# Row maxima of attention scores: at every second split tile, scores of key differences go through ScalarE before VectorE reduces them, and two sets of keys are kept, not three

## The chip, the cores and the metric

The kernel runs on one core of one Trainium2 chip. The metric is the device time of one execution in microseconds (us). The engines are called PE (TensorE's matmuls), PEld (its weight loads), DVE (VectorE), ACT (ScalarE), POOL (GpSimd) and SP (SyncE, which issues the DMAs).

## The reference

The input `x` is 8 sequences of 1024 tokens with 256 features, all in fp32. The work is one attention layer and one feed-forward layer, each with a layer norm before it, a layer norm after it and a residual:

```python
x = x + _layernorm(_L0_attn_ref(_layernorm(x), Wq, Wk, Wv, Wo))
x = x + _layernorm(_L0_ffn_ref(_layernorm(x), weight, alpha, bias))
# attention: 16 query heads and 4 key/value heads of 16 features, rotary embedding on q and k
scores = jnp.einsum('bhqd,bhkd->bhqk', q, k) / jnp.sqrt(jnp.float32(D))
p = jax.nn.softmax(scores, axis=-1)
o = jnp.einsum('bhqk,bhkd->bhqd', p, v)
```

What matters here is the softmax. Its row maximum has to be known before the exponentials are taken, so every score is computed twice: once to find the maximum of its row, and once, shifted by that maximum, for the exponential.

## The kernel before, in words

**Units and blocks.** The kernel walks through 16 units (half a sequence of queries, 512 tokens, index `u`; two units make a sequence `b`). A unit has 4 blocks (index `i`, 64 in all) and a block has 8 steps of 4 exponentials. A unit is thus 32 steps or 128 exponentials, and the kernel has 2048 exponentials.

**The two score streams.** For an exponential, PE writes a 128x512 tile `se` of scores (L655), ACT takes `Exp` of it into `e` (L671), and PE multiplies `e` with `v_aug` into `av` (L691). `se` tiles come from a pool of 3 PSUM banks, which the products of projections and tails share. For the maxima, PE writes score tiles `sm` (L582, in `max_scores`); one holds 2 x 512 scores of 128 queries, one half for each half of the keys, and spans two PSUM banks. There are 2 such tiles in turn. DVE reduces a tile with `TENSOR_REDUCE` (L607, in `reduce_halves`) into `mx`. The maxima run 13 steps ahead of the exponentials. When a block has its maxima, DVE joins them (`mc`, L624), PE transposes them (`pm`, L630), ACT and DVE split them (`mh`, `ml`, L632 and L639), and a DMA writes them as extra rows into the stacked queries `q_st` (L646), so that the second score product comes out shifted.

**Windows.** The order on PE, DVE and ACT is written by hand, in windows (`window`, from L1114). A window has 3 exponentials, or 2 where a part of the projection or of the tail with a PSUM product of its own is ready. For each exponential PE also does one half of an `sm` tile (a pair of matmuls, one `se` and one `sm`). After the pairs come the part's product, if any, and the `av` products of the window before the last. A window that ends after the first half of an `sm` tile leaves a split tile: `reduce_early` (L612) has DVE reduce the first half by itself at the end of the window, and the second half is reduced by itself after the first pair of the next window. So a whole tile is one `TENSOR_REDUCE` of 128x1024, and a split tile is two of 128x512.

**Projections and keys.** While unit `u - 3` runs, unit `u` is projected: `kv_and_dram` makes keys and values and sends the keys through DRAM into another layout; `kt` rotates them on POOL, splits them into a high and a low part, writes them to DRAM (`dk`) and at once calls `stack_keys`, whose six DMAs load them into `k_st` (L481). There are three sets of `k_st` and `v_aug`, one for each sequence in turn. `v` fills `v_aug`. `P_PARTS` (L942) lists at which step each part stands. DMAs are issued by SP in an order that a scheduler chooses.

**Tail.** The last unit's tail uses `k_st` and `v_aug` of finished sequences as scratch.

Of the kernel before, what the change touches and what calls it, by code (L numbers as in the profile page):

```python
# [16 lines left out]
P = 128  # L17
# [5 lines left out]
UQ = UT * P  # L23
EPS = 1e-5
THRESH_FACTOR = 0.7


@with_exitstack
def kernel(
# [103 lines left out]
    k_st, v_aug, q_st = [], [], []  # L133
    for i in range(2):
        q_st.append(const.tile([P, G, 2, UQ], F32R, name=f"q_st{i}"))
    for i in range(3):
        k_st.append(const.tile([P, 2, S], F32R, name=f"k_st{i}"))
        v_aug.append(const.tile([P, NK, HKV, 32], F32, name=f"v_aug{i}"))

# [10 lines left out]
    def fill_constant_parts(i):  # L150
        if i > 0:
            fill_rows(k_st[i], 1, NROW, 64 - NROW)
        nc.gpsimd.memset(v_aug[i], 1.0)

    def split_hi(eng, hi, src):
# [149 lines left out]
    class Project:  # L305
# [54 lines left out]
        def v(self):  # L360

            lo = 0 if self.u < 2 else DK
            pt = psum([P, UT, P], f"ptv_{self.u}")
            for t in range(UT):
                src = self.kv_t[lo:, t * P : (t + 1) * P]
                nc.tensor.transpose(pt[:, t, lo:], src, ident[lo:, lo:])
            if lo == 0:
                self.k_rot = qkp.tile([P, UT, DK], F32, tag="k_rot", name=f"k_rot_{self.u}")
                nc.scalar.copy(self.k_rot, pt[:, :, :DK])
            if self.u == 0:  # L370
                self.split_q(0, (0,))
            nc.scalar.copy(
                v_aug[self.b % 3][:, self.half * UT : (self.half + 1) * UT, :, 0:HD],
                pt[:, :, DK:].rearrange("p t (r d) -> p t r d", d=HD),
            )

# [30 lines left out]
        def kv_and_dram(self):  # L407

            u = self.u
            for p in range(2):  # L410
                self.kv(p)
            d_k = dram.tile([DK, UQ], F32, tag="d_k", name=f"d_k_{u}")
            nc.sync.dma_start(out=d_k, in_=self.kv_t[:DK])
            self.k_rot = qkp.tile([P, 2, P], F32, tag="k_rot", name=f"k_rot_{u}")
            src = d_k.rearrange("(m e) (g t) -> e g m t", e=2, t=P)
            for e in range(2):
                nc.sync.dma_start(out=self.k_rot[:, e, :], in_=src[e])

        def kt(self):
            rotate(  # L420
                self.eng, self.k_rot, cos_kt_sb[:, self.half], sin_kt_sb[:, self.half],
                work.tile([P, 2, P], F32, tag="t2k", name=f"t2k_{self.u}", bufs=1),
            )
            hl = qkp.tile([P, 2, 2, P], F32R, tag="k_parts", name=f"ks_{self.u}")
            split(self.eng, hl[:, 0], hl[:, 1], self.k_rot)
            dk = self.dk = dram.tile([2, DK, UQ], F32, tag="dk", name=f"dk_{self.u}")
            dst = dk.rearrange("l (m e) (g t) -> l e g m t", e=2, t=P)
            for l in range(2):
                for e in range(2):
                    nc.sync.dma_start(out=dst[l, e], in_=hl[:, l, e, :].bitcast(F32))  # L430
            self.stack_keys()

        def q_product(self, p):
            if self.q_rot is None:
# [36 lines left out]
                    src = self.hl["q"][64 * c : 64 * (c + 1), l].rearrange("p e t -> p (e t)")  # L471
                    nc.sync.dma_start(out=rows[l, c], in_=src.bitcast(F32))

        def stack_keys(self):

            keys = slice(self.half * UQ, (self.half + 1) * UQ)
            src = self.dk.rearrange("l (r a d) t -> a l d r t", a=2, d=HD)
            for a in range(2):
                for band, l in enumerate((0, 0, 1)):
                    row = 64 * a + HD * band  # L480
                    nc.sync.dma_start(  # L481
                        out=k_st[self.b % 3][row : row + HD, :, keys].bitcast(F32), in_=src[a, l]
                    )

    def row_pickers():

# [75 lines left out]
    def head_and_tile(i, r2, t):  # L562
        return r2 * UT + t if i // G < NU - 1 else 2 * t + r2

    def max_scores(v):


        i, k = divmod(v // 2, 2 * NK)
        u, part = i // G, v % 2
        if i == 0:  # L570
            a, ch, t, r2 = 1 - part, k // NK, k // 2 % UT, k % 2
        else:
            a, ch, t, r2 = 1 - k % 2, part, k // 4, k // 2 % 2
        queries = block_queries(i, r2)
        queries = queries[:, t * P : (t + 1) * P] if u < NU - 1 else queries[:, t]
        if part == 0:
            sm[0] = ps_mx.tile([P, 2, 512], F32, tag="sm", name=f"sm_{i}_{k}")
            if k == 0:
                mx[i] = small.tile([P, 2, 2 * UT, 2], F32, tag="mx", name=f"mx_{i}")
            reduced.clear()  # L580
        rows = slice(64 * a, 64 * a + 64)
        scores = nc.tensor.matmul(  # L582
            sm[0][:, part, :],
            queries[rows],
            k_st[(u // UPB) % 3][rows, r2, ch * 512 : (ch + 1) * 512],
            start=True,
            stop=True,
        )
        if part == 0:
            return  # L590
        if reduced:
            tc.declare_no_dep(scores.ins, early[0], reason="another bank")
        if i == 0:
            nc.vector.tensor_reduce(
                mx[i][:, ::-1, head_and_tile(i, r2, t), ch], sm[0], AX.X, ALU.max
            )
        else:
            reduce_halves(i, k, 2)
        if k == 2 * NK - 1:
            shift_join(i)  # L600
            due.append((v // 4 + (1 if i < 3 else 2), i))
# [10 lines left out]
    def reduce_early(v):  # L612

        i, k = divmod(v // 2, 2 * NK)
        if i > 0 and v % 2:
            reduce_halves(i, k, 1)

    sm, mhl, shifts, reduced, early = {}, {}, {}, [], [None]
# [32 lines left out]
    def exp_scores(n, r2, a, sc):  # L651
        i, kt = divmod(n, NK)
        queries = block_queries(i, r2)
        rows = slice(64 * a, 64 * a + 64)
        nc.tensor.matmul(  # L655
            sc if len(queries.shape) == 2 else sc.rearrange("p (j t) -> p j t", j=G),
            k_st[(i // G // UPB) % 3][rows, r2, kt * P : (kt + 1) * P],
            queries[rows],
            start=True,
            stop=True,  # L660
        )
# [20 lines left out]

    def av_piece(i, first, end):

        va = v_aug[(i // G // UPB) % 3]
        if first == 0:
            av_ps[0] = ps_av.tile([P, UQ], F32, tag="av", name=f"av_{i}")
        for kt in range(first // UQ, (end - 1) // UQ + 1):
            lo, hi = max(first - kt * UQ, 0), min(end - kt * UQ, UQ)
            for r in (1, 2, 3, 0):  # L690
                nc.tensor.matmul(  # L691
                    av_ps[0][32 * r : 32 * r + 32, lo:hi],
                    va[:, kt, r, :],
                    es[i * NK + kt, r // 2, r % 2][:, lo:hi],
                    start=(kt == 0 and lo == 0),
                    stop=(kt == NK - 1 and hi == UQ),
                )
# [140 lines left out]
    class LastTail(Tail):  # L838
# [4 lines left out]
        def __init__(self, u):  # L843
            super().__init__(u)
            self.xn = qkp.tile([P, UT, D], F32, tag="xn", name="xn_last", bufs=2)

        def new(self, what, p):
            i = (B - 3) % 3 if what == "x1" else (B - 2) % 3
            if what == "xn":
                return self.xn[:, p : p + 1]  # L850
            if what == "hl":
                tile = k_st[i][:, p // 2, (p % 2) * 2 * D : (p % 2 + 1) * 2 * D]
                return tile.rearrange("p (l t d) -> p l t d", l=2, t=1)
            return v_aug[i][:, 2 * p : 2 * p + 2].rearrange("p t r d -> p (t r d)").unsqueeze(1)
# [82 lines left out]
    def load(u):  # L937
# [3 lines left out]

    P_PARTS = (  # L942
        (26, "begin", 0), (33, "x", 0, 0), (34, "x", 0, 1), (37, "begin", 1), (43, "x", 1, 0),
        (45, "x", 1, 1), (49, "kv_and_dram"), (51, "q", 0), (52, "kt"), (53, "v"), (55, "q", 1),
        (57, "q_to_dram"),
    )
    L_PARTS = (
        (10, "n", 0), (13, "o", 0), (15, "attn", 0), (16, "stats_a", 0), (19, "stats_x", 0),
# [8 lines left out]
        (29, "x", 1, 1), (31, "ffn", 1), (31, "stats_f", 0), (33, "stats_f", 1),  # L957
    )

    P_FIRST = (47, 51, 52, 54, 57, 58, 59, 60, 62, 61, 63, 64)  # L960
    T_LAST = (1, 3, 4, 5, 9, 10, 11, 14, 17, 20, 21, 21, 22, 24, 25, 26, 23, 27)

    warm = []
# [13 lines left out]
    def third(name, *args):  # L977
        return lambda: getattr(projects[2], name)(*args)
# [6 lines left out]
    for k, fs in enumerate((  # L985
# [16 lines left out]
        [third("v"), second("split_q", 1), second("q_to_dram")],  # L1002
        [],
        [],
        [(fill_constant_parts, 2)],
        [],
        [third("q", 0)],
        [(behind_shift, 1, third("kt"))],
# [2 lines left out]
    )):  # L1011
        for f in fs:
            at(k - START, *(f if isinstance(f, tuple) else (f,)))
    for u in range(3, NU):
        start = SPU * (u - 4)
        steps = P_FIRST if u == 3 else [k for k, *_ in P_PARTS]
# [6 lines left out]
                at(k, stage)  # L1023
        at(start + steps[0] - 1, begin_project, u)
        for k, (_, *p) in zip(steps, P_PARTS):
            at(start + k, part, projects, u, *p)
    for u in range(2, NU):
        at(SPU * (u - 1) + 1, stack_queries, u)
    for u in range(NU - 1):
# [63 lines left out]

    def start_step(n):
        for q in range(4):
            max_scores(maxima[0])
            maxima[0] += 1
            if q == 1:
                take_low()
        collect(n)  # L1100
        do_parts(99)
# [12 lines left out]
    def window(s):  # L1114
# [8 lines left out]
        else:  # L1123
            end = min(maxima_by(s + size), 4 * NSTEP)
            for q in range(max(size, end - maxima[0])):
                if q < size:
                    exp_one(s + q)
                if maxima[0] < end:
                    max_scores(maxima[0])
                    maxima[0] += 1  # L1130
                if q == 0:
                    take_low()
# [143 lines left out]
```

## Time and profile before

| what | value |
|---|---|
| median of 3 runs | 1645.67 us (1642.97 to 1648.71) |
| profiled execution: time, span | 1642.63 us, 1640.8 us |
| granted TensorE clock, mean | 0.989 |
| busy share of the span: PE, DVE, ACT, POOL | 96%, 85%, 78%, 51% |
| `TENSOR_REDUCE` of 128x1024 / 128x512 (L607) | 712 / 592 |
| exponentials (L671) | 1996, mean 602 ns |

A row of the groups gives line, engine, operation, output and inputs, shape and count; then busy time in us and the mean duration of one in ns; then the engine's idle time just before them and what ended it. A row of the timeline gives start and duration in us; rows of one kind that follow each other are merged, with their count. A busy PE is not a PE at its peak, since matmuls are pipelined. The 52 exponentials that stand under another line belong to the end of the kernel, where no maxima are left.

### The profile page before, as it was taken

Reading aid. Unit: us, or ns where it says so; the run is one execution under the profiler, and the core shown is the slowest. Engines: PE = TensorE matmul, PEld = TensorE weight load, DVE = VectorE, ACT = ScalarE, POOL = GpSimd, SP = SyncE. Lnnn points to the kernel's source line nnn. Section 1 sums busy time; section 2 is a strip of 40 time slices with the busy share of each in tenths; the row PEclk is TensorE's granted clock in tenths of the full one; section 3 lists DMA queues with packets and bytes.
Section 4 is the critical chain, followed back from the end, with each engine's and each line's share of the span. In section 5 each row is a group of like instructions: output and inputs, shape, how many; then the busy total and the mean of one; then the engine's idle time right before and its main releaser. Section 6 shows DMA issues by size and latency. Waiting matters only on the chain.

```text
span 1640.8 us, 37250 instructions
## 1 busy us (share of the span) xinstructions
PE 1579.7 (96%) x14712; PEld 818.5 (50%) x14712; DVE 1399.3 (85%) x2049; ACT 1274.8 (78%) x2479; POOL 835.4 (51%) x1239
## 2 busy tenths in 40 slices
PE   7999999999999999999999999999999999999997
PEld 5544455454545545454544545455454544444544
DVE  7778788889898888989889898988989888898964
ACT  4657778878787887878788787887878787877884
POOL 5532457374653737455373835547374552323363
PEclk8989999999999999999999999999999999999999
DMA  4151425125151422515133251513325151231100
GB/s 139 53 101 34 91 77 101 59 76 101 56 106 49 91 67 82 101 46 105 60 83 75 77 106 44 104 49 89 71 67 104 40 97 42 46 70 34 42 15 27
DMA packets 86079, 117.99 MB, mean 72 GB/s; under 512 B 12088, under 2 KB 50808, under 8 KB 85752
## 3 DMA queue, kind: packets, MB, share of 16 engines
q1 hardware_dynamic: 85904, 115.60, 29.9%
q8 instruction: 116, 1.90, 0.5%
q14 instruction: 59, 0.48, 0.1%
HBM read 68.65 MB, written 45.88 MB: 70 GB/s over the span
## 4 chain that ended last, share of the span: by engine, by line
PE 80%; DVE 10%; DMA 3%; ACT 2%; POOL 2%; issue 2%; SPq 1%; POOLq 0%; DVEq 0%; ACTq 0%
PE av L691 28%; PE se L655 28%; PE sm L582 9%; DVE mx L607 7%; PE pa L283 3%; PE pq L283 2%; PE pf L283 2%; PE pt_ot L267 2%; ACT e L671 2%; PE pt_xt L267 2%; PE pkv L283 2%; DMA q_st<-ml 1%; DMA k_rot<-d_k 1%; PE pm L630 1%; DMA dk<-ks 1%
## 5 line engine op out<-in xcount | busy, mean ns | idle before, releaser
L607 DVE TENSOR_REDUCE mx<-sm 128x2 f32<-128x1024 f32 (+1 forms) x1304 | 1205.3, 973 | 191.9 <-PE sm L582 174.1
L671 ACT ACTIVATE e<-se 128x512 f32<-128x512 f32 x1996 | 1058.2, 602 | 223.0 <-PE sm L582 172.4
L582 PE MATMUL sm<-k_st,q_st 64*128 64x512 f32 x2048 | 748.4, 450 | 6.9 <-DVE mx L607 3.9
L655 PE MATMUL se<-q_st,k_st 64*128 64x512 f32 x2048 | 705.5, 441 | 26.7 <-ACT e L671 14.4
L691 PE MATMUL av<-e,v_aug 128*32 128x256 f32 (+3 forms) x8608 | 607.2, 378 | 0.0
L655 PEld LDWEIGHTS se<-q_st,k_st 64*128 64x128 f32 x2048 | 324.9, 185 | 405.7 <-ACT e L671 302.1
L582 PEld LDWEIGHTS sm<-k_st,q_st 64*128 64x128 f32 x2048 | 326.1, 185 | 65.1 <-DVE mx L607 41.9
L691 PEld LDWEIGHTS av<-e,v_aug 128*32 128x32 f32 x8608 | 194.4, 108 | 211.0 <-issue 148.3
L241 POOL TENSOR_SCALAR lnsc<-mv 128x2 f32<-128x2 f32 (+1 forms) x134 | 25.8, 193 | 400.1 <-DVE mv L239 395.1
L765 POOL TENSOR_TENSOR xn<-xn,a 128x512 f32<-128x512 f32 x30 | 38.4, 1282 | 131.8 <-DMA a<-d_rec 101.2
L826 POOL TENSOR_TENSOR a<-a,bias_bc 128x512 f32<-128x512 f32 x30 | 38.6, 1287 | 108.3 <-ACT a L825 108.3
L242 POOL TENSOR_TENSOR lnsc<-lnsc,mhalf 128x2 f32<-128x2 f32 (+1 forms) x134 | 92.5, 691 | 0.9
L162 POOL TENSOR_TENSOR hl<-xn,hl 128x512 fp32r<-128x512 f32 x60 | 76.5, 1287 | 0.4
L253 POOL TENSOR_SCALAR xn<-x,lnsc 128x256 f32<-128x256 f32 x116 | 65.1, 570 | 2.2
L237 DVE BATCH_NORM_STATS2 bnst<-a 128x6 f32<-128x256 f32 x120 | 44.5, 413 | 4.6 <-POOL a L826 4.6
L297 POOL TENSOR_TENSOR t<-q_rot,sin_q_sb 128x512 f32<-128x512 f32 x31 | 39.9, 1288 | 15.5 <-ACT q_rot L439 15.4
L283 PE MATMUL pa<-woh,hl 128*128 128x256 f32 x240 | 46.2, 294 | 1.1 <-ACT e L671 1.1
L283 PE MATMUL pq<-xt,wqkvh 128*128 128x256 f32 x256 | 45.8, 303 | 0.5 <-ACT e L671 0.5
L237 DVE BATCH_NORM_STATS2 bnst<-x 128x6 f32<-128x256 f32 x124 | 45.9, 412 | 0.4 <-DMA x<-in_L_attn_x 0.4
L271 ACT CAST ot<-pt_ot 128x512 fp32r<-128x512 f32 x66 | 39.6, 601 | 4.7 <-PE pt_ot L267 4.7
L439 ACT COPY q_rot<-pq 128x512 f32<-128x512 f32 x32 | 18.8, 586 | 30.9 <-PE pq L283 30.9
L162 POOL TENSOR_TENSOR hlq<-q_rot,hlq 128x512 fp32r<-128x512 f32 x31 | 39.8, 1285 | 4.8 <-ACT hlq L159 4.5
(157 smaller groups left out, 1303.1 us busy)
## 6 DMA issues: line engine op xcount, KB each, us to landing
q_st<-dq SPq DMA_DIRECT2D x90, 256.0 KB
dq<-hlq SPq DMA_DIRECT2D x60, 256.0 KB
d_av<-avsb SPq DMA_DIRECT2D x60, 256.0 KB
x<-in_L_attn_x SPq DMA_DIRECT2D x15, 512.0 KB
xn<-d_av SPq DMA_DIRECT2D x30, 256.0 KB
a<-d_rec SPq DMA_DIRECT2D x30, 256.0 KB
xr<-in_L_attn_x SPq DMA_DIRECT2D x15, 512.0 KB
out_x<-a SPq DMA_DIRECT2D x30, 256.0 KB
```

Of the source, the lines that this page charges most:

```text
L162: eng.tensor_tensor(lo, src, hi.bitcast(F32), ALU.subtract)
L237: nc.vector.bn_stats(st[:, t, :], src[:, t, :])
L242: nc.gpsimd.tensor_tensor(sc[:, 1, :], sc[:, 1, :], mhalf[:, :n], ALU.pow)
L253: eng.tensor_scalar(dst[:, t, :], src[:, t, :], sc[:, 0, t : t + 1] if eng is nc.gpsimd else mv[:, t, 0:1], sc[:, 1, t : t + 1], ALU.add i ...
L267: nc.tensor.transpose(pt[:, c, t * P : (t + 1) * P], src[:, t, c * P : (c + 1) * P], ident_r)
L283: nc.tensor.matmul(out, chunk(left[i], c), chunk(right[j], c), start=(k == 0), stop=(k == len(steps) - 1),)
L297: eng.tensor_tensor(dst, x, table.unsqueeze(1).to_broadcast(list(x.shape)), ALU.mult)
L582: scores = nc.tensor.matmul(sm[0][:, part, :], queries[rows], k_st[(u // UPB) % 3][rows, r2, ch * 512 : (ch + 1) * 512], start=True, stop= ...
L607: early[0] = nc.vector.tensor_reduce(mx[i][:, a, head_and_tile(i, r2, t), lo:n], sm[0][:, lo:n, :], AX.X, ALU.max).ins
L655: nc.tensor.matmul(sc if len(queries.shape) == 2 else sc.rearrange("p (j t) -> p j t", j=G), k_st[(i // G // UPB) % 3][rows, r2, kt * P : ...
L671: nc.scalar.activation(e, sc, AF.Exp, scale=1.0 / D**0.5)
L691: nc.tensor.matmul(av_ps[0][32 * r : 32 * r + 32, lo:hi], va[:, kt, r, :], es[i * NK + kt, r // 2, r % 2][:, lo:hi], start=(kt == 0 and lo ...
```

## The change

Of the split tiles, every second one takes another way, for blocks of sequences 1 to 7 apart from each sequence's first block. Its first half is not the scores with the first half of the keys: it is the scores with `k_df`, the keys of the second half minus those of the first. Its second half is the scores with the first half of the keys. ACT takes the positive part (`Relu`) of the first half into an SBUF tile `rest` at the end of the window, behind the window's exponentials, and in place of both reductions DVE adds `rest` to the second half and takes the maximum of the sums in one instruction, since max(s0, s1) = s0 + relu(s1 - s0).

`k_df` is made on POOL once a sequence, from the rotated keys of both units (`k_differences`), goes through DRAM as the keys do (`dkd`), and is loaded by six DMAs 9 steps before the exponentials reach the sequence (`stack_differences`). To have room for `k_df` and `rest`, `k_st` and `v_aug` have two sets. So `stack_keys` is no longer called by `kt`: it stands at its own step, 68, as `v` does at 67, when the set's former sequence is done. `kt` stands at 54. `kt`, `q_to_dram`, `stack_keys` and `stack_differences` are issued behind the latest shift rows' DMA. Each `mx` tile is first filled by POOL with a large negative number, as only one of its two columns is written for such a tile. The last tail gets a tile of its own for `x1`.

```diff
+    k_df = const.tile([P, 2, S // 2], F32R, name="k_df")
-    for i in range(3):
+    for i in range(2):
         k_st.append(const.tile([P, 2, S], F32R, name=f"k_st{i}"))
...
+        def k_differences(self):
+            first = projects[self.u - 1].k_rot
+            self.eng.tensor_tensor(first, self.k_rot, first, ALU.subtract)
+            self.dkd = self.k_to_dram("dkd", first)
...
+    def maxima_tile(i):
+        if i < NU * G and i not in mx:
+            mx[i] = small.tile([P, 2, 2 * UT, 2], F32, tag="mx", name=f"mx_{i}")
+            nc.gpsimd.memset(mx[i], LEAST)
...
-    def max_scores(v):
+    def max_scores(v, end):
...
+            if v + 1 == end and u >= UPB and i % (UPB * G) > 0:
+                sm["turn"] = not sm.get("turn", False)
+                if sm["turn"]:
+                    sm["rest"] = work.tile([P, 512], F32, tag="rest", name=f"rest_{i}_{k}")
+                    keys = k_df
+        elif sm["rest"] is not None:
+            keys = k_st[(u // UPB) % 2][:, :, :512]
...
-        if reduced:
+        if reduced or sm["rest"] is not None:
             tc.declare_no_dep(scores.ins, early[0], reason="another bank")
...
+        elif sm["rest"] is not None:
+            rest, x = sm["rest"], head_and_tile(i, r2, t)
+            nc.vector.tensor_tensor_reduce(
+                rest, sm[0][:, 1, :], rest, 1.0, LEAST, ALU.add, ALU.max, mx[i][:, a, x, 0:1]
+            )
...
-        if i > 0 and v % 2:
+        if v % 2 and sm["rest"] is not None:
+            early[0] = nc.scalar.activation(sm["rest"], sm[0][:, 0, :], AF.Relu).ins
+        elif i > 0 and v % 2:
             reduce_halves(i, k, 1)
...
-        (45, "x", 1, 1), (49, "kv_and_dram"), (51, "q", 0), (52, "kt"), (53, "v"), (55, "q", 1),
-        (57, "q_to_dram"),
+        (45, "x", 1, 1), (49, "kv_and_dram"), (51, "q", 0), (54, "kt"), (55, "q", 1),
+        (57, "q_to_dram"), (67, "v"), (68, "stack_keys"),
...
+    at(8 - START + 10, third("stack_keys"))
+    for u in range(3, NU, UPB):
+        at(SPU * (u - 4) + (66 if u == 3 else 55), part, projects, u, "k_differences")
+        at(SPU * (u - 1) - 9, behind_latest, part, projects, u, "stack_differences")
```

## The prediction

> **What bounds the kernel now.** I read the page first: busy shares, then the chain that ended last.
>
> ```profile
> PE 1579.7 (96%) x14712; PEld 818.5 (50%) x14712; DVE 1399.3 (85%) x2049; ACT 1274.8 (78%) x2479; POOL 835.4 (51%) x1239
> ...
> PE 80%; DVE 10%; DMA 3%; ACT 2%; POOL 2%; issue 2%; SPq 1%; POOLq 0%; DVEq 0%; ACTq 0%
> ```
>
> PE is on the chain for most of the time; DVE has a tenth of it, ACT almost nothing. DVE is busier than ACT, but neither is full. So a DVE microsecond is worth something only where PE waits for it. The groups by shape give the prices, and a row of the waits (us in sum, times, longest) tells who stands for whom:
>
> ```profile
> L607 DVE TENSOR_REDUCE mx<-sm 128x2 f32<-128x1024 f32 x712 | 855.3, 1216 | 167.5 <-PE sm L582 153.2 <-PE se L655 11.0
> L607 DVE TENSOR_REDUCE mx<-sm 128x1 f32<-128x512 f32 x592 | 381.9, 680 | 24.5 <-PE sm L582 20.9
> ...
> L639 DVE SCALAR_TENSOR_TENSOR ml<-mh,low,pm 32x128 fp32r<-32x128 f32 x64 | 21.0, 327 | 3.1 <-ACT mh L632 3.1
> ...
> L162 DVE TENSOR_TENSOR xs<-xn,xs 128x512 fp32r<-128x512 f32 x3 | 3.1, 1045 | 0.0
> ...
> L797 DVE TENSOR_TENSOR v_aug<-v_aug,xr 128x256 f32<-128x256 f32 x3 | 1.3, 426 | 0.1
> L881 DVE TENSOR_TENSOR xn_last<-po,rec 128x256 f32<-128x256 f32 x3 | 1.3, 425 | 0.1
> ...
> L510 DVE TENSOR_SCALAR low<-low 32x1 f32<-32x1 f32 x1 | 0.1, 142 | 0.0
> ```
>
> ```profile
> PEld sm L582 <- DVE mx L607: 41.9, 127, 1.4
> ...
> PE se L655 <- DMA q_st<-ml: 9.9, 8, 3.1
> ```
>
> Last the timeline, engine by engine, at one split tile between two windows of three. This is the place where the change acts:
>
> ```profile
> 687.58 1.20 DVE L607 TENSOR_REDUCE mx<-sm 128x2 f32<-128x1024 f32 x1
> 688.72 1.20 DVE L607 TENSOR_REDUCE mx<-sm 128x2 f32<-128x1024 f32 x1
> 689.85 0.67 DVE L607 TENSOR_REDUCE mx<-sm 128x1 f32<-128x512 f32 x1
> 690.62 0.69 DVE L607 TENSOR_REDUCE mx<-sm 128x1 f32<-128x512 f32 x1
> 691.23 1.21 DVE L607 TENSOR_REDUCE mx<-sm 128x2 f32<-128x1024 f32 x1
> ...
> 688.65 1.62 ACT L671 ACTIVATE e<-se 128x512 f32<-128x512 f32 x3
> 690.59 3.27 ACT L671 ACTIVATE e<-se 128x512 f32<-128x512 f32 x6 [0.32 <-PE sm L582]
> ...
> 688.84 0.50 PE L582 MATMUL sm<-k_st,q_st 64*128 64x512 f32 x1
> ...
> 690.05 0.73 PE L582 MATMUL sm<-k_st,q_st 64*128 64x512 f32 x2
> ...
> 692.50 0.49 PE L582 MATMUL sm<-k_st,q_st 64*128 64x512 f32 x1
> ```
>
> The third pair's `sm` half at 688.84 starts 0.06 us after the reduction of the tile two before it ends (687.58 + 1.20 = 688.78): DVE holds PE there, and again at 692.50 (691.23 + 1.21 = 692.44). But between the two halves DVE is early: the first half is reduced by 690.52, and the second waits until 690.62 for PE. What frees the tile is the end of the second half's reduction, 691.31, and that hangs on PE's pair at 690.05, not on DVE's load.
>
> **The change part by part.** The built program has the same PE instructions, 112 of the 296 split tiles on the new way: 65 between two windows of three, 34 between a window of three and one of two, 13 behind a window of two. Each loses two DVE reductions of 128x512; it gets one ACT instruction, one DVE instruction of 128x512 and one DVE instruction of 128x1 that reads the accumulator.
>
> *DVE's instructions.* Back to back, DVE rows overlap by some 0.07 us (687.58 to 688.72 with 1.20), so two halves take 2 x 0.60 = 1.20 us of DVE. The new sum has no row. The sum of a PSUM and an SBUF operand at 128x256 (L881) takes 425 ns, and 256 elements more cost (1216 - 680)/2 = 268 ns: 0.69 us. Its bounds are 0.67, a half's reduction, and 1.045 (L162, at the start of the kernel); I take 0.69, as L881 has its very operands. The accumulator read lies between 0.06 (142 ns less the overlap) and 0.33 (L639); I take 0.12, nearer to the smallest row. So DVE's work falls by 112 x (1.20 - (0.69 - 0.08 + 0.12)) = 53 us. This is not the gain, because of when it can start.
>
> *When it can start.* The positive part stands on ACT behind the window's exponentials. In the timeline they end at 688.65 + 1.62 = 690.27; a further instruction of that shape starts 0.10 earlier and takes 0.60 (L671's mean is 602 ns): until 690.77. The sum can start at about 690.8, ends at 691.49, and with the read DVE is done at 691.6. Before, it was done at 691.31. The tile comes free 0.3 us later, the next reduction starts 0.3 later, and the pair at 692.50 moves by 0.3. That window has an extra copy on ACT ahead of its exponentials (`avsb`, 0.60 us); without it the sum would wait for PE's second half instead (690.05 + 0.50 = 690.55), and be done at 691.4: 0.1 later. In the window that follows (691.75), DVE would be done 0.15 later, but the next pairs on these buffers have 0.36 us to spare: nothing. Laid over all 161 such split tiles of the trace, the positive part ends after DVE has become free in 130 and PE's second half comes last in 29; the median tile is released 0.2 us later, and PE feels about 0.15 on average. So: 65 x 0.15 = 9.8 us. Ahead of a window of two with a product of its own, the product (0.5 to 1.7 us on PE) hides most of it: 34 x 0.05 = 1.7. Behind a window of two ACT is done early: 13 x 0 = 0. If the cover of these 47 were gone they would cost 47 x 0.15 = 7.
>
> *ACT.* An additional instruction costs ACT 0.49 us from start to start (three in 1.57 us in most windows: (1.57 - 0.60)/2). Ahead of a window's first exponential ACT stands idle for 0.32 us at 690.59, and 0.36 to 0.43 in the windows around it, waiting for PE. That hides all but some 0.1 us, and `se` banks are freed with some 0.4 us to spare: 112 x 0.02 = 2 us. ACT's total, 1275 + 55 of 1641, stays short of full. At this place a rule speaks against the change. The row first: ACT makes a 128x512 tile in 602 ns, DVE reduces one in 680. The Trainium skill (ScalarE: Activation LUTs, Rules for kernel authors) says that relu, max and add belong on VectorE, not on ScalarE. By the row the single operation is cheaper on ACT by 0.08 us; by the rule the move would be a loss in itself. Neither of them prices ACT's queue, which costs more here.
>
> *Accumulation.* L881 and L797 take the same time with one operand in PSUM and with both in SBUF, so nothing in these rows slows a sum of two tensors. The Trainium skill (Vector Engine (DVE) Microarchitecture Reference, Points that are easy to get wrong) states that such an accumulating operation runs at half rate with two SBUF sources that are not bf16. Here one source lies in PSUM, and no row shows the case; by that rule the instruction would take 2 x 0.54 + 0.15 = about 1.2 us, and the change would cost 65 x 0.5, some 33 us, more.
>
> *Keys and DMAs.* Two sets of keys: the old set is done at step 64 of a projection, and the keys are stacked at 68, while the maxima need them 15 steps later or more. A step is 3.0 us (first exponential at 63.2, last at 1620.4, 512 steps): hidden by 45 us. `k_df` is loaded at 9 steps and needed at 4 steps before the sequence; 15 us less some 6 for `dk` and the six loads (0.63 us each on SP): hidden; without that cover PE stands a few us, 7 times. POOL gains 7 x 1.9 us (0.73, 0.41 and 0.73 for tiles of that size from 626 to 630) and 64 small fills, off the path at 51%. In the built order the shift rows' DMA now stands ahead of the key loads; before, one waited behind six of them (438.44 to 442.6) and PE stood for it. The waits of this kind after 400 us sum to about 3 us: I take back 2.5.
>
> *Sum.* 9.8 + 1.7 + 2 - 2.5 = +11 us on the profiled 1642.6 (span 1640.8 and 1.8 around it): 1653.6. The median of the runs lies 3 us above that execution, so the forecast for it is 1657.
>
> **The rivals.** *DVE's relief counts (faster).* In units 13 and 14 no projection runs, windows of three follow each other and DVE has hardly a gap, 19.1 us busy from 1345 to 1365. Over 200 to 1600 us the third pair's `sm` trails its `se` by 75 us in sum. The new way has 112 of 296 split tiles; if it takes away half of their share, 75 x 0.38 / 2 = 14 us go: 1632. It decides if the positive part is there before DVE gets to the tile; in the timeline it comes 0.9 us late (690.77 against 689.85). Where statistics stand on DVE between the halves (1345.40 to 1346.36 in the trace), it is in time, so some of this is real. *All hidden (same).* The tile comes 0.1 later, and the 0.4 us of room at most pairs takes it up; the shift rows give back the rest: 1646. *The sum is slow (slower).* At 1.045 us the release is 0.35 later still: 65 x (0.15 + 0.35) + 34 x 0.1 = 36, 1681; with the read at 0.33 too, 65 x 0.7 + 34 x 0.25 = 54, 1700. It decides from a sum of about 0.9 us. *The keys come late:* a stall of 4 us each, 28 us, 1674 alone; against it stand the 9 us of room.
>
> **How the numbers follow.** Forecast 0.50, slow sum or late keys 0.10, same 0.16, relief 0.24. A measurement of this kernel can tell about 0.3% (5 us) from no change. Slower by more: 0.50 + 0.10 = 0.60; within: 0.16; faster: 0.24. The forecast's own range is 1652 to 1663, with PE held by 0.08 to 0.25 at the 65 tiles. The likeliest cases have both signs, so the range runs from 1631, just past the relief's 1632, to 1681, the slow sum's.
>
> **What would show it.** Right: DVE's busy time falls by 40 to 55 us, its idle time before the sum, ended by ACT, grows by as much, the release of such tiles comes 0.1 to 0.3 us late, waits of `sm` for DVE do not shrink. Wrong: sums that start at once after DVE's own reduction, windows of three that get shorter in units 13 and 14, or a sum far from 0.7 us.

## The result and the profile after

The changed kernel takes 1661.11 us in the median of 4 runs (1660.14 to 1667.02), against 1645.14 us for the kernel before, timed beside it: a ratio of 1.0102, 95% interval 1.0072 to 1.0133. It is slower by about 17 us. The profiled execution is 1660.19 us with a span of 1658.4, at a granted clock of 0.987.

The page after, busy shares and chain:

```profile
PE 1593.7 (96%) x14712; PEld 825.7 (50%) x14712; DVE 1342.9 (81%) x2049; ACT 1319.8 (80%) x2591; POOL 850.2 (51%) x1323
...
PE 79%; DVE 8%; ACT 5%; DMA 3%; POOL 2%; issue 2%; SPq 0%; POOLq 0%; DVEq 0%
```

DVE has lost 56.4 us of work and ACT has got 45.0; on the chain DVE gave up two points and ACT took three. The groups by shape and the waits that answer to those of before:

```profile
L642 DVE TENSOR_REDUCE mx<-sm 128x2 f32<-128x1024 f32 x712 | 857.8, 1218 | 177.8 <-PE sm L616 157.4 <-PE se L692 16.7
L642 DVE TENSOR_REDUCE mx<-sm 128x1 f32<-128x512 f32 x368 | 240.8, 683 | 24.2 <-PE sm L616 22.1 <-PE se L692 1.1
...
L629 DVE CUSTOM_DVE_ANT_0 rest<-sm,rest 128x512 f32<-128x512 f32 x112 | 77.5, 692 | 60.8 <-ACT rest L651 36.9 <-PE sm L616 13.2 <-ACT mh L669 7.7
...
L651 ACT ACTIVATE rest<-sm 128x512 f32<-128x512 f32 x112 | 70.0, 625 | 0.0
```

```profile
PEld sm L616 <- DVE mx L642: 42.5, 146, 1.4
DVE rest L629 <- ACT rest L651: 36.9, 66, 0.9
PE se L692 <- DMA q_st<-ml: 13.4, 4, 5.5
```

The sum has its row now (`CUSTOM`, 692 ns). PE's wait for `sm` tiles has not shrunk with DVE's work. The waits for shift rows are fewer and longer. The place that the prediction showed, by PE's pair 10.80 us later in this trace (700.85 for 690.05), in the timeline:

```profile
701.53 0.69 DVE L629 CUSTOM_DVE_ANT_0 rest<-sm,rest 128x512 f32<-128x512 f32 x1 [0.81 <-PE sm L616]
702.14 0.08 DVE L629 DVE_READ_ACCUMULATOR2_ANT mx<- 128x1 f32 x1
702.14 1.22 DVE L642 TENSOR_REDUCE mx<-sm 128x2 f32<-128x1024 f32 x1
...
700.85 0.73 PE L616 MATMUL sm<-k_st,q_st 64*128 64x512 f32 x2
...
699.21 1.62 ACT L708 ACTIVATE e<-se 128x512 f32<-128x512 f32 x3
700.65 0.67 ACT L651 ACTIVATE rest<-sm 128x512 f32<-128x512 f32 x1
```

The Relu ends at 701.32, the sum starts at 701.53, and DVE is done at 702.22: 691.42 on the clock of before, where it was 691.31. What ended DVE's idle time here is not the Relu but PE's second half, which starts at 700.85 and takes 0.50 us. Of all 112 sums, the Relu ended the idle time of 66 and PE's `sm` that of 18.

**Where the time went.** From the first exponential of a unit to that of the next (128 exponentials, us):

| kernel | first exponential | units 0, 1 | units 2 to 12 | units 13, 14 | rest |
|---|---|---|---|---|---|
| before | 63.2 | 114.4, 99.2 | 96.2 to 97.3 | 92.9, 92.9 | 115.0 |
| after | 62.0 | 118.0, 101.8 | 97.8 and 97.3 in turn | 94.6, 93.6 | 115.2 |

Up to the start of unit 2 the change costs 5.1 us, though it has no new tile there: the first of them is in block 9. Units 2 to 12 cost 10.0 us, the rest 2.5. Each row is one execution, and the start differs from one to the next: the eight kernels here that share the changed kernel's beginning start unit 2 at 279.0 to 283.6 us.

### The profile page after: what moved, and what is told of

Read it like the earlier page. It is cut to its first block, busy times and chain, and to the rows that moved or that the text cites. A ratio compares the mean times of both kernels' runs of the same rounds, so it can differ in the third digit from the quotient of the medians.

```text
span 1658.4 us, 37617 instructions
## 1 busy us (share of the span) xinstructions
PE 1593.7 (96%) x14712; PEld 825.7 (50%) x14712; DVE 1342.9 (81%) x2049; ACT 1319.8 (80%) x2591; POOL 850.2 (51%) x1323
## 4 chain that ended last, share of the span: by engine, by line
PE 79%; DVE 8%; ACT 5%; DMA 3%; POOL 2%; issue 2%; SPq 0%; POOLq 0%; DVEq 0%
PE av L728 28%; PE se L692 27%; PE sm L616 10%; DVE mx L642 6%; ACT e L708 3%; PE pa L286 3%; PE pq L286 3%; PE pf L286 2%; PE pt_ot L270 2%; PE pt_xt L270 2%; PE pkv L286 1%; DMA q_st<-ml 1%; DMA d_av<-avsb 1%; PE pm L667 1%; ACT rest L651 1%
## 5 line engine op out<-in xcount | busy, mean ns | idle before, releaser
L642 DVE TENSOR_REDUCE mx<-sm 128x2 f32<-128x1024 f32 (+1 forms) x1080 | 1077.9, 1036 | 202.0 <-PE sm L616 179.5
L692 PE MATMUL se<-q_st,k_st 64*128 64x512 f32 x2048 | 722.6, 448 | 25.1 <-DMA q_st<-ml 13.4
L616 PE MATMUL sm<-k_st,q_st 64*128 64x512 f32 x1936 | 724.0, 456 | 5.5 <-DVE mx L642 2.7
L692 PEld LDWEIGHTS se<-q_st,k_st 64*128 64x128 f32 x2048 | 330.2, 186 | 399.8 <-ACT e L708 279.8
L616 PEld LDWEIGHTS sm<-k_st,q_st 64*128 64x128 f32 x1936 | 311.8, 186 | 56.0 <-DVE mx L642 33.4
L629 DVE CUSTOM_DVE_ANT_0 rest<-sm,rest 128x512 f32<-128x512 f32 x112 | 77.5, 692 | 60.8 <-ACT rest L651 36.9
L651 ACT ACTIVATE rest<-sm 128x512 f32<-128x512 f32 x112 | 70.0, 625 | 0.0
L616 PE MATMUL sm<-k_df,q_st 64*128 64x512 f32 x112 | 47.2, 421 | 1.9 <-DVE mx L642 0.3
```

What stands on the lines that cost most here:

```text
L616: scores = nc.tensor.matmul(sm[0][:, part, :], queries[rows], keys[rows, r2], start=True, stop=True)
L629: nc.vector.tensor_tensor_reduce(rest, sm[0][:, 1, :], rest, 1.0, LEAST, ALU.add, ALU.max, mx[i][:, a, x, 0:1])
L642: early[0] = nc.vector.tensor_reduce(mx[i][:, a, head_and_tile(i, r2, t), lo:n], sm[0][:, lo:n, :], AX.X, ALU.max).ins
L651: early[0] = nc.scalar.activation(sm["rest"], sm[0][:, 0, :], AF.Relu).ins
L692: nc.tensor.matmul(sc if len(queries.shape) == 2 else sc.rearrange("p (j t) -> p j t", j=G), k_st[(i // G // UPB) % 2][rows, r2, kt * P : ...
```

## The experiments

The ratio is to before, timed on the same chip. The first four kernels share a chip (before: 1646.9 us in the median), the next four another (1645.6), the last four a third (1644.3), so medians of different groups compare to some 3 us; where it matters, the ratios are given too. "Unit" is the length of a middle unit in the profile.

| kernel | median us | ratio, 95% interval | unit us |
|---|---|---|---|
| no_turns | 1656.3 | 1.0059 (1.0040 to 1.0079) | 97.2 |
| sum_not_waiting | 1661.75 | 1.0093 (1.0073 to 1.0112) | 97.3, 97.8 |
| sum_alone | 1648.83 | 1.0010 (0.9997 to 1.0023) | 96.4, 96.6 |
| start_mended | 1657.91 | 1.0062 (1.0044 to 1.0080) | 97.3, 97.8 |
| relu_alone | 1667.8 | 1.0145 (1.0124 to 1.0166) | 97.8, 98.3 |
| only_threes | 1656.8 | 1.0075 (1.0055 to 1.0095) | 97.1 |
| only_products | 1662.98 | 1.0106 (1.0090 to 1.0123) | 97.4, 97.9 |
| v_early | 1649.29 | 1.0025 (1.0014 to 1.0037) | 96.3 |
| values_late | 1687.88 | 1.0250 (1.0224 to 1.0276) | 99.0 to 104.4 |
| after_values | 1650.73 | 1.0036 (1.0023 to 1.0050) | 96.6, 96.7 |
| after_values_start | 1644.2 | 0.9994 (0.9980 to 1.0008) | 96.6 |
| rows_first | 1642.63 | 0.9983 (0.9972 to 0.9995) | 96.3 |

**No new tiles (no_turns).**

```diff
-                sm["turn"] = not sm.get("turn", False)
+                sm["turn"] = False
```

> The change without its 112 new tiles: every split tile has both halves reduced by DVE again, while the key differences are still made and stored, POOL still fills the maxima tiles, two sets of keys stand where three did. Theory T (the loss is the late sum at the new tiles, about 0.15 us at each of the 65 between windows of three, and a disturbed start, where the third unit's keys and differences stand ahead of shift rows on SP's queue): units 0 and 1 stay 6 us longer than before, units 2 to 15 go back to before's and keep the 3 us of the shift rows: 1647 us (1645 to 1650). Rival K (the stores, loads and fills of the differences cost along the whole kernel): 1653 to 1660. Rival R (the new tiles are a relief, and hide a larger loss of the rest): above 1661.

Measured: 1656.3, 9 us over before. That is rival K's number: more than half of the loss has nothing to do with the new tiles. (Its cause is not K's: v_early, below, has the stores, loads and fills too, and its middle units are short.) The middle units take 97.1 to 97.3 us (but for one of 98.2), where before takes 96.3 if no shift row is late. The 0.9 us are lost in every unit, while the differences are made in every second one only.

**The sum without its wait (sum_not_waiting).**

```diff
-                rest, sm[0][:, 1, :], rest, 1.0, LEAST, ALU.add, ALU.max, mx[i][:, a, x, 0:1]
+                dump, sm[0][:, 1, :], cos_q_sb[:, :512], 1.0, LEAST, ALU.add, ALU.max, mx[i][:, a, x, 0:1]
```

> At the 112 new tiles ACT still takes the positive part of the first half, but DVE's sum adds a table of constants to the second half, and so does not wait for ACT (the maxima of these tiles are wrong by that; the tile itself is still released only when both have read it). Theory T (DVE's wait for the Relu is the price): DVE's idle time ended by that Relu, 37 us after, is gone; 8 to 14 us less than after, 1647 to 1653 us. Rival A (the price is ACT's own 0.62 us at each tile, which puts the next exponentials off): as after, 1658 to 1663. Rival P (the price is the release of the tile by the Relu, late in ACT's queue, whether DVE waits or not): as after too, with PE's wait for the tile now put down to ACT.

Measured: 1661.75. But the edit did not do what it says. The group's row in this kernel:

```profile
L629 DVE CUSTOM_DVE_ANT_0 dump<-sm,cos_q_sb 128x512 f32<-128x512 f32 x112 | 77.5, 692 | 61.0 <-ACT rest L651 38.5 <-PE sm L616 12.7 <-ACT mh L669 7.7
```

The sum still waits for ACT: where the Relu ended its idle time (70 tiles, 66 in the changed kernel), it starts 0.03 us after the Relu's end, as there. So the run tells nothing about the wait; it only shows that the table in place of `rest` changes nothing.

**The sum without the Relu (sum_alone).** As above, and the Relu goes, with its tile `rest`:

```diff
-            early[0] = nc.scalar.activation(sm["rest"], sm[0][:, 0, :], AF.Relu).ins
+            pass
```

> At the 112 new tiles the Relu is left out, and DVE's sum adds a table of constants to the second half (the maxima of these tiles are wrong by that): DVE's relief by itself, without ACT's load and without the wait. Theory T: as sum_not_waiting or up to 3 us less, 1644 to 1652 us; if DVE's relief is worth anything at all, below no_turns. Rival A (ACT's own time): 8 to 14 us under sum_not_waiting. Rival P (the release): also 8 to 14 us under sum_not_waiting, with PE's waits for the tile shorter than before's. That the relief is worth nothing: equal to no_turns within 2 us.

Measured: 1648.83, 7.5 us under no_turns. DVE's relief by itself does count, and the Relu with all that hangs on it costs 12 to 13 us.

This run also shows what a wait for two engines adds. Where PE's second half ended DVE's idle time, the sum starts 67 ns after that matmul's end (median of 38 sums, a time modelled by the profile) when PE is all it waits for, and 177 ns after it in the changed kernel (median of 18), where it waits for the Relu too.

**The Relu by itself (relu_alone).** DVE reduces both halves; ACT has the 112 Relus for nobody.

```diff
+        if v % 2 and sm["extra"] is not None:
+            nc.scalar.activation(sm["extra"], cos_q_sb[:, :512], AF.Relu)
+        if i > 0 and v % 2:
             reduce_halves(i, k, 1)
```

> DVE reduces both halves of every split tile, with the plain keys, as in no_turns; at the 112 tiles ACT takes a Relu of 128x512 from a table in SBUF into a tile that nobody reads: ACT's load by itself, with no release and no wait for it. Nothing is left out of the result. The runs so far put the Relu of the changed kernel at +13 us (sum_not_waiting less sum_alone). Theory A (the price is ACT's own 0.6 us, which puts the exponentials behind it off): as much over no_turns, 1669 us (1664 to 1674). Rival P (the price is the tile's release by the Relu, late in ACT's queue): as no_turns, 1656 us (1653 to 1659).

Measured: 1667.8, 11.5 us over no_turns by the medians and 14 by the ratios, with a Relu of 648 ns each. Theory A holds and rival P falls: ACT's own time is enough to lose what the Relu loses.

**Place by place.** These kernels have the same order on PE, so their exponentials can be laid over each other. The table gives how many us the eleven exponentials from the start of a new tile's window take more than in no_turns, as the median over units 2 to 12; a place is named by the exponential of the unit at which its window starts.

| place | tiles | next window | after | relu_alone | sum_alone |
|---|---|---|---|---|---|
| 10 | 11 | two, product | 0.10 | 0.13 | -0.01 |
| 22 | 11 | three | -0.54 | 0.00 | -0.59 |
| 38 | 11 | three | 0.13 | -0.01 | 0.01 |
| 58 | 11 | three | 0.14 | 0.16 | 0.00 |
| 74 | 6 | three | -0.08 | 0.00 | -0.22 |
| 85 (behind a two) | 6 | three | 0.00 | 0.01 | 0.00 |
| 98 | 6 | two, product | 0.49 | 0.51 | 0.00 |
| 110 | 11 | two, product | 0.10 | 0.12 | 0.00 |
| 122 | 11 | three | 0.21 | 0.24 | 0.00 |

Over these 84 tiles the sums are +4.1 (after), +10.1 (Relu) and -7.8 us (relief). DVE's relief is worth something at two places of nine, and there much. The Relu costs at five. At 10, 58, 98, 110 and 122 the Relu ends 0.4 to 0.7 us after PE's second half and the sum is late by that, yet the changed kernel loses there no more than relu_alone, where no sum waits. At 38 and 74 neither part loses, but both together lose 0.13 or 0.14: only there does the sum's later start show. At 74 the Relu ends 0.43 us after PE's half. At 38 it has ended just before PE's half, and what is late is the start by itself, 177 ns after PE's half in the place of 67.

**Two kinds of place (only_threes, only_products).** The new tiles are put at listed places only:

```diff
-                sm["turn"] = not sm.get("turn", False)
+                sm["turn"] = (i, k) in TURNS
```

> The change with its 65 new tiles between two windows of three exponentials alone; the other 47 are reduced by DVE as before. Nothing is left out. Theory W (a fit of the traces' exponentials, window by window, against no_turns: relief and Relu cancel here, -0.15 and +0.14 us at each): as no_turns, 1656 us (1653 to 1658). The theory on record (0.15 us lost at each of these): 1664 to 1667.

> The change with its 34 new tiles ahead of a window of two that holds a product alone. Nothing is left out. Theory W (0.20 us lost at each, the relief being worth nothing there): 6.8 us over no_turns, 1663 us (1660 to 1665), the waits of PE that ACT's exponentials end above no_turns. The theory on record (0.05 us at each): 1657 to 1659.

Measured: 1656.8 and 1662.98, against 1656.3 without new tiles. Theory W's numbers come, and the theory on record has it the wrong way round: the 65 tiles between windows of three cost nothing in sum (0.5 us by the medians, 2.6 by the ratios, within their intervals; the middle units are 97.1 us against 97.2), the 34 ahead of a product cost 7 us. One sign of W's is missing: PE's waits that ACT's exponentials end do not grow (the largest row from 290 to 1550 us has 230.0 us, 230.6 in no_turns). How the time goes is seen at place 98 in the timelines of ACT, each with PE's third `se` of the window that follows. no_turns:

```profile
549.52 1.57 ACT L708 ACTIVATE e<-se 128x512 f32<-128x512 f32 x3 [0.62 <-PE sm L616]
550.97 0.60 ACT L741 COPY avsb<-av 128x512 f32<-128x512 f32 x1
551.43 1.13 ACT L708 ACTIVATE e<-se 128x512 f32<-128x512 f32 x2
552.40 0.64 ACT L274 CAST ot<-pt_ot 128x512 fp32r<-128x512 f32 x1
553.06 1.57 ACT L708 ACTIVATE e<-se 128x512 f32<-128x512 f32 x3
...
553.10 0.49 PE L692 MATMUL se<-q_st,k_st 64*128 64x512 f32 x1
```

only_products, 4.57 us later:

```profile
554.09 1.58 ACT L715 ACTIVATE e<-se 128x512 f32<-128x512 f32 x3 [0.63 <-PE sm L623]
555.53 0.62 ACT L658 ACTIVATE rest<-sm 128x512 f32<-128x512 f32 x1
556.01 0.62 ACT L748 COPY avsb<-av 128x512 f32<-128x512 f32 x1
556.48 1.14 ACT L715 ACTIVATE e<-se 128x512 f32<-128x512 f32 x2
557.44 0.66 ACT L274 CAST ot<-pt_ot 128x512 fp32r<-128x512 f32 x1
...
558.15 0.50 PE L699 MATMUL se<-q_st,k_st 64*128 64x512 f32 x1
```

ACT has no gap here: the `avsb` copy, two exponentials and the product's copy all move by 0.47 us. The product `pt_ot` and the `se` tiles share three PSUM banks, and a bank is free when ACT has read it. So PE's third pair of the window that follows starts at 558.15, not at 553.10 + 4.57 = 557.67. In both traces it starts 0.05 to 0.06 us after the product's copy ends (553.04 and 558.10).

**The values (v_early, values_late).** First no_turns with the values' transposes back at step 53 (with a third `v_aug`, which that needs):

```diff
-        (45, "x", 1, 1), (49, "kv_and_dram"), (51, "q", 0), (54, "kt"), (55, "q", 1),
-        (57, "q_to_dram"), (67, "v"), (68, "stack_keys"),
+        (45, "x", 1, 1), (49, "kv_and_dram"), (51, "q", 0), (53, "v"), (54, "kt"),
+        (55, "q", 1), (57, "q_to_dram"), (68, "stack_keys"),
```

> no_turns with a third set of the values' tiles, so that a unit's values are transposed at step 53 again, between its two q products, and not at step 67 in the next unit; keys stay at two sets, the differences and the fills stay. Nothing is left out. no_turns has 97.2 us in each middle unit of 128 exponentials, before has 96.3 where no shift row is late. Theory V (the 0.9 us of each unit are the moved values, whose four transposes now take a place among the next unit's windows): middle units of 96.3 us, 10 to 12 us less than no_turns, 1645 us (1643 to 1648). Rival F (the 0.9 us are POOL's fills, the key parts' DMAs or the moved key rotation): as no_turns, 1656 us (1653 to 1659).

Measured: middle units of 96.3 us in all of 2 to 12, as theory V has it, 10.5 us less than no_turns over these units; the median is 1649.29, not 1645, since the start takes part of it back. In the profiled execution the first exponential comes at 67.5 us and units 0 and 1 take 7.3 more than before. The two late shift rows of the changed kernel's start are there (PE waits 2.5 us at 127 and 5.7 at 212); what else delays this start is open. Then the reverse, before with the values at 67:

```diff
-        (45, "x", 1, 1), (49, "kv_and_dram"), (51, "q", 0), (52, "kt"), (53, "v"), (55, "q", 1),
-        (57, "q_to_dram"),
+        (45, "x", 1, 1), (49, "kv_and_dram"), (51, "q", 0), (52, "kt"), (55, "q", 1),
+        (57, "q_to_dram"), (67, "v"),
```

> The kernel before with one thing moved: the four transposes of a unit's values from step 53 to step 67, where the change put them; three sets of keys and values, no differences, no fills, no new tiles. Nothing is left out. Theory V (no_turns lost 0.9 us in each middle unit by this move): 97.2 us in the middle units where before has 96.3 to 97.1, 7 to 11 us more than before, 1655 us (1652 to 1657). Rival F (the loss came from the fills, the key parts or the two sets, and v_early mended it in another way): 1645 us, as before.

Measured: 1687.88, far beyond both (the profiled execution, 1693.85, is the slowest of six). The step does what V says (PE's waits for the values' bank are those of no_turns, 4.4 us in 11 times), and more: the order on PE has moved against SP's queue, and the shift rows come late once a unit. PE's waits from 290 to 1550 us and SP's timeline at the longest of them:

```profile
PE se L655 <- DMA q_st<-ml: 26.7, 11, 4.5
...
PE ptv L366 <- ACT e L671: 4.4, 11, 0.4
```

```profile
949.49 2.36 SPq L430 DMA_DIRECT2D dk<-ks  x4
952.79 3.44 SPq L481 DMA_DIRECT2D k_st<-dk  x6
956.34 1.41 SPq L646 DMA_DIRECT2D q_st<-ml  x2
```

DVE had made these shift rows (`ml`) by 949.52. They stood for 6.8 us behind the key parts and six key loads, and PE stood for 4.45. In the changed kernel these DMAs are issued behind the newest shift rows; so that order is worth not the 3 us that before loses, but far more once the values stand at 67: no_turns, with both, takes 31 us less.

**One new tile a unit (after_values).** `TURNS` holds place 22 alone, 11 tiles.

> The change with 11 new tiles alone, the one in each unit that begins at its exponential 22, in the window of three behind the moved values' transposes. Nothing is left out. Theory W (in only_threes the exponentials regain 0.53 us against no_turns at each of these places, and lose 0.1 to 0.2 at most of the others): 6 us under no_turns, 1650 us (1648 to 1653), middle units of 96.7 us. Rival (a new tile is worth the same wherever it stands between windows of three, about nothing): as no_turns, 1656 us.

Measured: 1650.73; middle units of 96.6 to 96.7. The places' table holds. no_turns at this place, DVE and then PE (the first window of three behind the values' transposes; the first row holds a whole tile and the first half of the split one):

```profile
588.87 1.82 DVE L642 TENSOR_REDUCE mx<-sm 128x2 f32<-128x1024 f32 x2 [1.08 <-PE sm L616]
590.61 0.74 DVE L240 BATCH_NORM_STATS2 bnst<-x 128x6 f32<-128x256 f32 x2
591.27 0.30 DVE L242 BATCH_NORM_AGGREGATE mv<-bnst 128x2 f32<-128x6 f32 x2
591.49 4.19 DVE L642 TENSOR_REDUCE mx<-sm 128x1 f32<-128x512 f32 x4
...
591.38 0.49 PE L692 MATMUL se<-q_st,k_st 64*128 64x512 f32 x1
592.20 0.49 PE L616 MATMUL sm<-k_st,q_st 64*128 64x512 f32 x1 [0.33 <-DVE mx L642]
```

after_values, 1.13 us later:

```profile
590.00 1.23 DVE L647 TENSOR_REDUCE mx<-sm 128x2 f32<-128x1024 f32 x1 [1.10 <-PE sm L621]
591.14 0.74 DVE L240 BATCH_NORM_STATS2 bnst<-x 128x6 f32<-128x256 f32 x2
591.80 0.30 DVE L242 BATCH_NORM_AGGREGATE mv<-bnst 128x2 f32<-128x6 f32 x2
592.04 0.69 DVE L634 CUSTOM_DVE_ANT_0 rest<-sm,rest 128x512 f32<-128x512 f32 x1
...
592.51 0.50 PE L697 MATMUL se<-q_st,k_st 64*128 64x512 f32 x1
592.79 0.50 PE L621 MATMUL sm<-k_st,q_st 64*128 64x512 f32 x1
```

Statistics of 1.0 us stand on DVE between the halves. Without the first half's reduction ahead of them, the second half comes 0.58 us earlier, and PE's `sm` trails its `se` by 0.28 us and not by 0.82. The Relu is ready before that (0.18 us before the sum starts, in the median of these places). Of the 0.9 us that the moved values cost a unit, this tile gives back 0.54. What is left, 0.3 to 0.4, is of the size of PE's wait for the values' bank (4.4 us in 11 units); I did not test that by itself.

**The start (start_mended, after_values_start).**

```diff
-    at(8 - START + 10, third("stack_keys"))
+    at(16, behind_latest, third("stack_keys"))
...
-        at(SPU * (u - 4) + (66 if u == 3 else 55), part, projects, u, "k_differences")
+        at(SPU * (u - 4) + (76 if u == 3 else 55), *([behind_latest] if u == 3 else []), part, projects, u, "k_differences")
```

and `bufs=8` for `mx`.

> The change as it is, with three places of the start moved: the third unit's key loads behind the shift rows of block 2, the first differences behind those of block 6, and eight maxima tiles in place of four, so that POOL's fills wait for no join. Nothing is left out. Theory T (of the 16 us lost, 5 are two waits of PE for shift rows at 121 and 206 us, which these loads held up): 1656 us (1654 to 1658), PE's waits for q_st<-ml back at 7 us or less before 260 us. Rival S (the start's loss is made good later, or another wait takes its place): 1660 to 1662.

> after_values with the three moves of start_mended. Nothing is left out. If the places' sum holds (3 to 5 us for the start, 6 for the eleven tiles): 1647 us (1644 to 1649), as before within what a measurement tells. If the start's gain and the tiles' do not add: 1650 or more.

Measured: 1657.91, 3 us under after by the medians and 0.4%, 6.6 us, by the ratios; and 1644.2, as before, 6.5 under after_values. SP's timeline of the changed kernel has the reason:

```profile
96.59 11.12 SPq L493 DMA_DIRECT2D k_st<-dk  x6
109.61 0.35 SPq L749 DMA_DIRECT2D d_av<-avsb  x1
111.53 4.47 SPq L485 DMA_DIRECT2D dq<-hlq  x4
116.11 2.40 SPq L683 DMA_DIRECT2D q_st<-ml  x2
```

The key loads of the third unit hold SP for 11 us, the query parts come after them, and the shift rows, ready on DVE at 111.84, are issued at 116.11; PE waits 4.16 us at 121.1 where before did not wait. With the loads moved, this wait is gone, and unit 2 starts at 276.1 and 276.2 us in the two kernels (before 276.8, after 281.8). The two gains add. The other wait that theory T named stays: PE waits 4.53 us at 200 (5.46 at 206 in after, 3.06 before), and its waits for shift rows before 260 us sum to 8.3 us, where the theory had 7 or less (13.4 in after, 7.0 before).

**Shift rows first (rows_first).** The kernel before, with key parts, query parts and key loads issued behind the newest shift rows from the fourth unit on, and the key loads at step 68:

```diff
+            behind = [behind_latest] if p[0] in ("kt", "q_to_dram", "stack_keys") else []
+            at(start + k, *behind, part, projects, u, *p)
```

> The kernel before with only the order of DMAs changed from the fourth unit on: key parts, query parts and key loads are issued behind the newest shift rows, the key loads eleven steps later. No new tiles, three sets, values where before has them. Nothing is left out. Theory (the shift rows that came 0.4 to 0.9 us late in before's middle units no longer do): 96.3 us in every middle unit, 3 us less, 1642 us (1640 to 1644). Rival (something else is late by then at the same places): as before, 1645 us.

Measured: 96.3 us in every middle unit, 3.5 us less over units 2 to 12; median 1642.63, ratio 0.9983. It has the lowest median of the kernels here, though its interval overlaps that of after_values_start: the one gain of the change that needs no new tile. In the profiled execution units 0 and 1 take 2.4 us more than before, so not all of it reaches the total.

## Why the prediction was right or wrong

The forecast, 1657 us with 0.60 on slower, came out on the right side, 4 us low. That is luck in good part: its sum was near the result by errors that cancel.

- *DVE's instructions: right.* The sum takes 692 ns (0.69 in the working), its read 83 ns (0.12), DVE lost 56 us (53; the sign named 40 to 55). L881, from which the 0.69 was taken as having the very operands, is a product with a broadcast operand in the code and not a sum; the size came out all the same. The half rate that the Trainium skill states for the two-tensor accumulating form with two SBUF sources that are not bf16 (Vector Engine (DVE) Microarchitecture Reference, Points that are easy to get wrong) was not tried here: this sum has one source in PSUM, and takes 692 ns, not 1.2 us.
- *"When it can start": the wait is there, but not at the tile shown, and the price is wrong.* The Relu ended DVE's idle time before 66 of the 112 sums, 36.9 us in all (the sign had as much as DVE's work falls, 56). At the tile shown, which is place 38, the Relu was over when PE's second half came, and the tile came free 0.11 us late (0.3 foretold), by the slower start of a sum that waits for two engines; the exponentials lost 0.13. Behind a window of two nothing was lost, as foretold (0.00 at place 85). But "65 x 0.15 = 9.8" is about 0 in the runs (only_threes): place 22 gains 0.54 each, which the working had only as a remark under a rival (statistics between the halves), and the losses at 58 and 122 are ACT's, not the sum's. The sum's later start shows at 38 and 74, 17 tiles x 0.13 = 2 us.
- *"The product hides most of it: 34 x 0.05 = 1.7": the step that failed in its reasoning.* It is 7 us. A product is no cover against ACT: it needs a PSUM bank that ACT frees.
- *"ACT: 112 x 0.02 = 2 us": the term most mis-sized,* 11.5 us or more measured by itself (the 7 us ahead of products are part of it). The 0.3 to 0.4 us of ACT's idle time were taken from one place for all. In no_turns ACT's first idle time behind the place is 0.55 us at 38, where the Relu costs nothing, but 0.26 at 58 and 0.20 at 122 (it costs 0.16 and 0.24), and at 98 none is left ahead of the product's copy (0.51); 0.30 and 0.41 at 10 and 110 do not hide it either (0.13 and 0.12). At 22 it is 0.20 too and the Relu is free, for there PE waits for DVE. As to the rule of the Trainium skill (ScalarE: Activation LUTs, Rules for kernel authors) that relu belongs on VectorE: no run here has a Relu on VectorE. The Relu on ACT takes 625 ns, the half's reduction whose place it takes 683 on DVE, and the change lost on ACT all the same, through its queue.
- *"This is not the gain": too hard.* The relief alone is worth 7.5 us (sum_alone against no_turns), half of the relief rival's 14, and all of it at two places. The rival's other sign did not come: units 13 and 14 got longer (94.6 and 93.6 us, before 92.9 each).
- *"Keys and DMAs: hidden": wrong twice.* Keys and differences are in time in the middle units, but at the start they hold up shift rows (some 5 us in the profile). And the list of what two sets move left out the values: `v` at 67 instead of 53 costs 0.9 us a unit, some 10 us, next to the Relu the largest loss of the change. It was in the diff, and I gave it no price.
- *Shift rows, -2.5: right in size,* 3.5 over the middle units in rows_first.

By the runs: the moved values +10 to 11, start +3 to 5, shift rows -3.5, relief -7.5, Relu +12 to 13: some 14 to 18 us, against 16 to 17 measured.

## What to carry to other kernels

Price everything that a change moves to make room, not only what it is about: here a buffer set less moved four small transposes, and that cost more than the new tiles did. An instruction moved to a less busy engine is priced by the place, from what stands ahead of and behind it in that engine's queue; a mean idle share says little, and nine places gave prices from -0.54 to +0.49 us. Before calling a wait removed, look at the row: the instruction may still wait for the same semaphore.

## What the runs showed of the hardware

A late DMA can cost PE more than the wait. Around the end of the wait of 4.45 us in values_late, at 958.46, the granted clock is down to half for 6.8 us (957.9 to 964.7), and the windows view of that trace (us, then busy time and instructions of PE, PEld, DVE, ACT and POOL, granted clock, DMA share, GB/s) shows it:

```profile
959.00:961.00 2.00, 2.00 (x10) 1.40 (x7) 1.28 (x2) 1.08 (x2) 1.10 (x1) 0.50 0.01 4
961.00:963.00 2.00, 2.00 (x16) 1.55 (x18) 0.82 (x4) 0.43 (x1) 0.00 (x0) 0.50 0.38 95
...
966.00:970.00 4.00, 4.00 (x43) 2.16 (x42) 3.71 (x6) 3.84 (x8) 4.00 (x7) 1.00 0.17 66
```

`se` matmuls take 0.76 us there and 0.49 before it. In the changed kernel the clock is at half for 13.7 us (119.0 to 132.7) around the end of the wait of 4.16 us at 121. Of the eleven late shift rows of values_late in the middle units (1.8 to 4.5 us), seven (1.88 to 4.45 us) had 3.4 or 6.8 us at half clock at their end or up to 2 us behind it and four (1.80 to 2.36 us) had none, so these runs give no sharp bound. It helps to explain how 24 us more of waits in values_late took 46 us from units 2 to 12, some 10 of them by the moved values: 31 us at half clock there can have cost up to 15, an estimate by the lost half.

A DVE instruction that waited for two engines started later than one that waited for PE alone, even with the other engine done, in the medians: 177 ns after the modelled end of PE's matmul (18 sums in the changed kernel), against 67 ns (38 sums in sum_alone). Where ACT was last, it started 32 ns after ACT's instruction (66 sums). Why, these runs do not show.
